# A spectral layer's last stage: tokens of a block spread over 128 partitions instead of 64

## The chip, the cores and the metric

The kernel runs on one core of a Trainium2 chip. The metric is the device time of one execution in microseconds (us); the kernel before took 10307.53 us, the median of three runs (10305.58 to 10308.48).

## The reference

Two layers of a "metaformer" work on `x` of shape (4, 64, 64, 128): 4 images, 4096 tokens each, 128 channels. Layer 0 is a selective-scan block and a mixture of experts; layer 1 is a message-passing block and a spectral one. Only the end of the last block matters here: a causal convolution of every channel with 16 filters along the tokens, done by discrete Fourier transforms, mixed by matrices, scaled, and added to its input.

```python
def _stu_conv(phi, u, n):
    Vf = jnp.fft.rfft(phi, n=n, axis=0)
    Uf_p = jnp.fft.rfft(u, n=n, axis=1)
    Uf_m = jnp.fft.rfft(u * sgn3, n=n, axis=1)
    U_plus = jnp.fft.irfft(Vf[None, :, :, None] * Uf_p[:, :, None, :], n=n, axis=1)[:, :sl]
    U_minus = jnp.fft.irfft(Vf[None, :, :, None] * Uf_m[:, :, None, :], n=n, axis=1)[:, :sl]
    ...
    for i, frac in enumerate((1, 2, 4, 8)):
        xi = x[:, :T // frac]
        si = _stu(xi, sigma, phi, M_u[i], M_phi_plus[i], M_phi_minus[i])
        ...
    return jnp.sum(stacked * weights, axis=-1)
...
t = t + _L1_ffn_ref(_ln_t(t), ...)
```

The weights are one-hot over the four lengths (all tokens, a half, a quarter, an eighth), so in the end each token's spectral result is multiplied by one number that depends only on which of four segments the token lies in.

## The kernel before, in words

The kernel first does the scans of the four images with everything else dealt in beside them, then the experts and sums of the last image, then `to_slots`, `spectrum()` (L1433) and `endings()` (L1586). `spectrum()` and `endings()` are the last calls.

The transform over 4096 tokens is split: a token's number is 64 times its block `j` (0 to 63) plus its position `p` in the block (0 to 63). `NB` = 64 blocks, `BP` = 64 positions, `NQ` = 64 frequencies with two parts each. `spectrum()` leaves in DRAM the array `zd` of shape (frequency q, part r, position p, image b, channel), 16.8 MB in float32; its last step (L1564) stores `zd` for the last two frequencies.

`endings()` undoes the transform over the blocks. For each position `p` it multiplies a constant matrix `gi_t` (128 rows: part and frequency; 64 columns: block) with the 128 x 512 slice of `zd` for that position (512 = 4 images x 128 channels), giving 64 blocks x 512 in PSUM. VectorE then multiplies by `wpj`, one number per block, and adds the block's residual `x3`; the sum goes to the output. It works in 16 groups of 4 positions:

- `load_x(g)` (L1596, DMAs at L1599): four DMAs, one per image, of 128 KB each. `mine` gives the rows: 64 blocks, each with 4 neighbouring tokens, 2 KB contiguous in DRAM. The tile `xr3` has the order (block, position, image, channel), so in SBUF each row falls apart into 512 B pieces.
- `load(g)` (L1601, DMAs at L1604): two DMAs of 512 KB, one per part, each onto 64 partitions of the tile `zb`, with 8 KB rows.
- `turn(g)` (L1609): four matmuls of 128 x 64 by 128 x 512 (L1612) and four `scalar_tensor_tensor` (L1614) on 64 partitions.
- `put(g)` (L1616, DMAs at L1618): four DMAs of 128 KB, back in the rows of `load_x`.

All these DMAs are issued on SP's queue, in an order that the framework's scheduler makes out of the loop: four x groups ahead, spectral loads two groups ahead of their use, puts one group behind. There are six `xr3` buffers, four `zb` buffers and eight PSUM banks. A seventh `load_x` reuses the first buffer and so waits for the first put to have landed, and so on.

`_dft_constants()` makes the matrices on the host: `gi_t`'s content and `seg`, a 64 x 4 mask that says which of the four segments each block lies in. `seg` is read in the tail of the filters' work, where it is multiplied by the segment weights and summed to `wpj` (L741 to L744).

Of the kernel before, what the change touches and what calls it, by code (L numbers as in the profile page):

```python
# [10 lines left out]
F32 = mybir.dt.float32  # L11
# [6 lines left out]
P = 128  # L18
B, H, W, C = 4, 64, 64, 128
# [21 lines left out]
BP = 64  # L41
NB = L // BP
NQ = NB
# [4 lines left out]
def _dft_constants():  # L48


    j, q = np.arange(NB)[:, None], np.arange(NQ)[None, :]
    th = 2 * np.pi / (2 * NB) * (j * q)
    one = (q == 0) & (j >= 0)
    alt = np.where(j % 2 == 0, 1.0, -1.0) * np.ones((1, NQ))
    co, si = np.cos(th), np.sin(th)
    fwd = np.stack([co, np.where(one, alt, -si)], 1)
    back = np.stack([np.where(one, 1.0, 2 * co), np.where(one, alt, -2 * si)], 1) / (2 * NB)
    gi = np.moveaxis(back, 0, 2)

    seg = np.zeros((NB, 4))  # L60
    for i in range(NB):
        seg[i, 0 if i < NB // 8 else 1 if i < NB // 4 else 2 if i < NB // 2 else 3] = 1.0
    r = fwd.reshape(NB, 2 * NQ), gi.reshape(2 * NQ, NB), seg
    return [np.ascontiguousarray(x.astype(np.float32)) for x in r]


# [35 lines left out]
def kernel(  # L102
# [35 lines left out]
    nc = tc.nc  # L138

    const = ctx.enter_context(tc.tile_pool(name="const", bufs=1))  # L140
# [3 lines left out]
    x3_d = [dram.tile([L, C], F32, name=f"x3_d{b}") for b in range(B)]  # L144
# [3 lines left out]
    zd = dram.tile([NQ, 2, BP, B, C], F32, name="zd")  # L148
# [64 lines left out]
    mu_t = wp.tile([P, 3, C], F32, name="mu_t")  # L213
    wseg = wp.tile([P, 4], F32, name="wseg")
    fu_c, gi_c, seg_c = _dft_constants()
    fq_c, gq_c = _twiddled()
    fq_d = nc.inline_tensor(fq_c, name="dft_in").ap()
    gq_d = nc.inline_tensor(gq_c, name="dft_out").ap()
    fu_t = wp.tile([NB, P], F32, name="fu_t")
    nc.sync.dma_start(fu_t, nc.inline_tensor(fu_c, name="dft_u").ap())  # L220
    gi_t = const.tile([P, NB], F32, name="gi_t")
    nc.sync.dma_start(gi_t, nc.inline_tensor(gi_c, name="dft_back").ap())
    wpj = const.tile([NB, 1], F32, name="wpj")

    eps5 = wp.tile([P, 1], F32, name="eps5")
    nc.vector.memset(eps5, 1e-5)
# [30 lines left out]
    def bank(shape, name):  # L257

        settle(1)
        return side["ones"].tile(shape, F32, name=name, tag="ps")  # L260
# [443 lines left out]
    def filters():  # L704

        with tc.tile_pool(name="fl", bufs=2) as fp:
# [30 lines left out]
            for s in range(2, -1, -1):  # L737
                nc.vector.tensor_add(
                    wseg[:, s : s + 1], wseg[:, s + 1 : s + 2], wt[:, 3 - s : 4 - s]
                )  # L740
            sg4 = fp.tile([NB, 4], F32, name="sg4")  # L741
            nc.sync.dma_start(sg4, nc.inline_tensor(seg_c, name="dft_seg").ap())
            nc.vector.tensor_mul(sg4, sg4, wseg[0:NB, :])
            nc.vector.reduce_sum(wpj, sg4, axis=AX.X)  # L744

            nc.scalar.activation(sg, sg, AF.Ln)
# [5 lines left out]
            for src, acc in ((m_plus, accp), (m_minus, accm), (m_u, mu_t)):  # L752
                n = src.shape[1]
                for i in range(4):
                    for k in range(0, n, 4):
# [4 lines left out]
                        h = hard[:, i : i + 1]  # L760
# [6 lines left out]
            for k in range(0, KF, 4):  # L767
# [11 lines left out]
                for a, m in enumerate((me, mo)):  # L779
                    ps = bank([P, 4, C], "mt_ps")  # L780
# [9 lines left out]
        with tc.tile_pool(name="hd_w", bufs=2) as hp:  # L790
# [21 lines left out]
            for k in range(0, KF, 4):  # L812
                ps = bank([BP, 4, 2, NQ], "h_ps")
                for i in range(4):
# [4 lines left out]
                        start=True,  # L819
                        stop=True,  # L820
# [11 lines left out]
            for q in range(0, NQ, 4):  # L832
# [5 lines left out]
                ps = bank([KK, 4, 2 * BP], "v_ps")  # L838
                for i in range(4):
                    for r in range(2):  # L840
# [4 lines left out]
                            start=(r == 0),  # L845
                            stop=(r == 1),
# [738 lines left out]

    def endings():  # L1586

        with tc.tile_pool(name="gi", bufs=3) as gp, tc.tile_pool(
            name="gi_ps", bufs=8, space=PSUM
        ) as gps:  # L1590
            zb, xr = {}, {}

            def mine(t, b, g):
                return t[b].rearrange("(j p) c -> j p c", j=NB)[:, 4 * g : 4 * g + 4, :]

            def load_x(g):  # L1596
                xr[g] = gp.tile([NB, 4, B, C], F32, name="xr3", bufs=6)
                for b in range(B):
                    nc.sync.dma_start(xr[g][:, :, b, :], mine(x3_d, b, g))  # L1599

            def load(g):  # L1601
                zb[g] = gp.tile([P, 4, B * C], F32, name="zb", bufs=4)
                for r in range(2):
                    nc.sync.dma_start(  # L1604
                        zb[g][r * NQ : (r + 1) * NQ],
                        zd[:, r, 4 * g : 4 * g + 4].rearrange("q p b c -> q p (b c)"),
                    )

            def turn(g):  # L1609
                for t in range(4):  # L1610
                    ps = gps.tile([NB, B * C], F32, name="gi_ps", tag="ps")
                    nc.tensor.matmul(ps, gi_t, zb[g][:, t, :], start=True, stop=True)  # L1612
                    xt = xr[g][:, t].rearrange("j b c -> j (b c)")
                    nc.vector.scalar_tensor_tensor(xt, ps, wpj, xt, ALU.mult, ALU.add)  # L1614

            def put(g):  # L1616
                for b in range(B):
                    nc.sync.dma_start(mine(out, b, g), xr[g][:, :, b, :])  # L1618

            for g in range(4):  # L1620
                load_x(g)
            n = BP // 4
            for g in range(n + 3):
                if g + 4 < n:
                    load_x(g + 4)
                if g < n:
                    load(g)
                if 0 <= g - 2 < n:
                    turn(g - 2)
                if 0 <= g - 3 < n:  # L1630
                    put(g - 3)

    def run(pieces):
        for _ in pieces:
# [3 lines left out]
    def beside(b):  # L1638

        if b == 0:  # L1640
            yield from before_scans(1)
            yield from before_scans(2)
            yield from gate(0)
            yield from gate(1)
            yield from filters()
            return
        if b == 2:
            yield from before_scans(3)
        yield from after_scans(b - 1)
        yield from experts_and_sums(b - 1)  # L1650
        yield from to_slots(b - 1)
        if b < B - 1:
            yield from gate(b + 1)

    with ExitStack() as c0:
# [113 lines left out]
        for s in range(-5, total + 2):  # L1769
            i = max(s, 0) // N  # L1770

            t = s + 5
# [8 lines left out]
            t = s + 3  # L1781
# [11 lines left out]
            if 0 <= s < total:  # L1793
                b, k, step, _ = chunks[i]
                n = s % N
# [44 lines left out]
            t = s - 1  # L1840
# [9 lines left out]
            t = s - 2  # L1850
            if t < 0:
                continue
            c, n = divmod(t, N)
            k = chunks[c][1]
            if n == 0:
                y = ys[c] = bps.tile([P, 4, 2, P], F32, name="y")
                if k == 0:
                    for q in range(4):
                        for h in range(2):
# [4 lines left out]
                                start=(q % 2 == 0 and h == 0),  # L1864
                                stop=False,
                                skip_group_check=True,
                            )
            for q in range(4):
                if q == 2:
                    deal(i_sp, i_act, i_pool, i_pe, i_dve)  # L1870
                for h in range(2):
# [5 lines left out]
                        start=(n == 0 and k > 0 and q % 2 == 0 and h == 0),  # L1877
                        stop=(n == N - 1),
# [31 lines left out]
    weights.close()  # L1910
    spectrum()
    endings()


# [72 lines left out]
```

## Time and profile before

| | us |
|---|---|
| median of three runs | 10307.53 |
| the profiled execution | 10298.26 |
| its span | 10296.2 |
| PE busy | 7631.4 (74% of the span) |
| DVE busy | 8537.4 (83%) |
| ACT busy | 6159.3 (60%) |
| POOL busy | 6493.4 (63%) |
| first DMA issue of `endings()` | at 10139.1 |
| first matmul of `endings()` | at 10161.5 |
| last VectorE instruction | at 10289.4 |
| 64 matmuls of L1612 (128 records) | 592 ns median a record |
| 64 instructions of L1614 | 743 ns median |
| DMA issue on SP at L1599, L1604, L1618 | 0.615, 0.614, 0.618 us median |

The profile is that of one execution. Busy shares are means over the whole span; stages differ, so a stage is read from the windows that cover it. A window's line gives busy time and count of each engine, then TensorE's granted clock as a share of full speed, the mean busy share of the 16 DMA engines (it can pass 1, since packets overlap), and what they moved in GB/s. A wait's line gives who waited, on what, how long in total, how often, and the longest.

### The profile page before, as it was taken

The numbers are of one execution on the slowest core, as the hardware profiler recorded it, in microseconds if no ns is written. First come the engines' busy times: TensorE is split into PE (matmuls) and PEld (weight loads), VectorE is DVE, ScalarE is ACT, GpSimd is POOL, SyncE is SP. The second block draws the span as 40 slices with busy tenths as digits, with TensorE's granted clock in tenths as the row PEclk, the third lists the DMA queues.
The fourth block names the chain that finished last, engine by engine and source line by source line (L and its number), as shares of the span: only waits on it lengthen the run. The fifth ranks groups of instructions, "written<-read, shape, count | busy, mean of one in ns | idle before, by whom it ended". The sixth has DMA issues, their size and how long they took to land. (4 is left out here: it accounts for less than half of the span.)

```text
span 10296.2 us, 137906 instructions
## 1 busy us (share of the span) xinstructions
PE 7631.4 (74%) x45570; PEld 4960.9 (48%) x45570; DVE 8537.4 (83%) x7103; ACT 6159.3 (60%) x11847; POOL 6493.4 (63%) x5948
## 2 busy tenths in 40 slices
PE   7676777667767767787767776767777767999996
PEld 3444444445543545444544554543555445666662
DVE  0899999989999999998999999999999951555553
ACT  4665766656755566675765666765576644554551
POOL 1677777878877778877877788877788741000000
PEclk9787787768777878788878887868877776999998
DMA  2556556657656645656756656756646663233336
GB/s 90 169 170 207 178 187 212 191 180 225 196 172 202 214 155 174 200 180 207 250 173 225 202 162 218 232 167 219 213 155 199 193 215 95 80 87 86 87 87 161
DMA packets 941918, 1806.03 MB, mean 175 GB/s; under 512 B 88184, under 2 KB 506648, under 8 KB 937624
## 3 DMA queue, kind: packets, MB, share of 16 engines
q1 hardware_dynamic: 941208, 1797.22, 54.7%
q8 instruction: 366, 6.00, 0.2%
q14 instruction: 344, 2.82, 0.1%
HBM read 1554.66 MB, written 242.22 MB: 175 GB/s over the span
## 5 line engine op out<-in xcount | busy, mean ns | idle before, releaser
L1846 POOL TENSOR_TENSOR hh<-hh,bc 128x1024 f32<-128x1024 f32 x2048 | 4886.8, 2386 | 384.9 <-DVE hh L1836 151.0
L1836 DVE TENSOR_TENSOR_SCAN hh<-da,hst,db 128x512 f32<-128x512 f32 x3584 | 4393.1, 1267 | 281.5 <-PE y L1872 30.1
L1872 PE MATMUL y<-ident,hh 128*128 128x128 f32 x16384 | 2723.2, 321 | 1524.8 <-POOL hh L1846 1429.0
L1786 ACT ACTIVATE da<-dl,aneg 128x512 f32<-128x512 f32 x4096 | 2781.8, 717 | 1543.7 <-DVE hh L1836 1531.2
L1872 PEld LDWEIGHTS y<-ident,hh 128*128 128x128 f32 x16384 | 2259.0, 166 | 2486.4 <-POOL hh L1846 1868.7
L1830 DVE TENSOR_TENSOR db<-du,bc 128x1024 f32<-128x1024 f32 x1920 | 2365.2, 1232 | 97.7 <-ACT du L1767 19.2
L1845 POOL COPY hst<-hh 128x2 f32<-128x2 f32 x1792 | 365.9, 204 | 1037.9 <-DVE hh L1836 937.0
L1495 PE MATMUL sp_ps<-vt,taps 32*128 32x256 f32 x8192 | 638.1, 405 | 52.3 <-DVE wt L1509 19.7
L1836 DVE TENSOR_TENSOR_SCAN hh<-da,db 128x512 f32<-128x512 f32 x512 | 597.0, 1208 | 38.4 <-PE y L1872 5.8
L1495 PEld LDWEIGHTS sp_ps<-vt,taps 32*128 32x128 f32 x8192 | 438.1, 185 | 245.6 <-DVE wt L1506 63.0
L440 PE MATMUL cv_ps<-xh,diag 128*128 128x512 f32 x1152 | 525.8, 599 | 1.8 <-ACT sg_v L382 0.9
L1524 PE MATMUL sp_ps<-wt,ut 128*32 128x256 f32 x8192 | 448.7, 379 | 45.2 <-DVE wt L1509 22.7
L1830 DVE TENSOR_TENSOR db<-dx,bc 128x1024 f32<-128x1024 f32 x128 | 179.3, 1401 | 297.9 <-POOL dx L1714 285.8
L1686 PE MATMUL dt_ps<-dts,dtw 8*128 8x512 f32 x512 | 378.9, 844 | 52.8 <-ACT sg_v L382 35.5
L1506 DVE COPY wt<-sp_ps 128x1024 f32<-128x1024 f32 x257 | 314.4, 1223 | 123.6 <-PE sp_ps L1495 112.2
L1509 DVE COPY wt<-sp_ps 128x1024 f32<-128x1024 f32 x255 | 311.3, 1221 | 121.9 <-PE sp_ps L1495 115.4
L1711 PE MATMUL dl_ps<-ex,ident 128*128 128x512 f32 x512 | 315.3, 704 | 121.9 <-POOL ex L1705 121.8
L1524 PEld LDWEIGHTS sp_ps<-wt,ut 128*32 128x32 f32 x8192 | 318.7, 110 | 172.6 <-ACT wt L1506 28.7
L1705 POOL TENSOR_TENSOR ex<-ex,dx 128x1024 f32<-128x1024 f32 x128 | 302.0, 2360 | 107.6 <-DMA bc<-bc_d 72.5
L1509 ACT COPY wt<-sp_ps 128x1024 f32<-128x1024 f32 x257 | 260.2, 1012 | 178.4 <-PE sp_ps L1495 169.4
L1456 DVE COPY zs<-sp_ps 128x1024 f32<-128x1024 f32 x128 | 156.5, 1222 | 241.8 <-PE sp_ps L1524 235.6
L1714 POOL TENSOR_TENSOR dx<-dl,xc 128x1024 f32<-128x1024 f32 x128 | 302.5, 2363 | 69.3 <-ACT dl L1712 62.8
(289 smaller groups left out, 9915.6 us busy)
## 6 DMA issues: line engine op xcount, KB each, us to landing
bc<-bc_d SPq DMA_DIRECT2D x2048, 512.0 KB
xc<-xc_d SPq DMA_DIRECT2D x128, 512.0 KB
y_d<-ys SPq DMA_DIRECT2D x128, 512.0 KB
w1t<-in_w_dram SPq DMA_DIRECT2D x96, 512.0 KB
w2t<-in_w_dram SPq DMA_DIRECT2D x192, 256.0 KB
xc_x<-xc_d SPq DMA_DIRECT2D x64, 512.0 KB
yk<-y_d SPq DMA_DIRECT2D x128, 256.0 KB
yk<-y_d SPq DMA_DIRECT2D x256, 128.0 KB
```

The lines of the kernel that those rows point to most:

```text
L440: nc.tensor.matmul(ps, diag[:, h, t, :], xh[:, 8 * g + dy : 8 * g + dy + 8, dx : dx + W], start=(t == 0), stop=(t == 8),)
L1495: nc.tensor.matmul(woven if (g // 2 + j) % 2 else plain, taps[rows, j, t, :], vt[i][rows].rearrange("k s n -> k (s n)"), start=True, stop= ...
L1509: copy()(dst, src)
L1524: nc.tensor.matmul(ps[32 * g : 32 * g + 32, k // 2, (k % 2) * 256 :][:, 0:256], w0.rearrange("d m u b -> d (m u b)"), wt[:, :, n : n + 2, ...
L1686: nc.tensor.matmul(ps, dtw[:, k, h * P : (h + 1) * P], dts, start=True, stop=True)
L1711: nc.tensor.matmul(ps, ident, t[:, h], start=t is dl, stop=t is w)
L1786: i_act = nc.scalar.activation(das[t][:, h, :], sizes[t // N][0][:, h, :], AF.Exp, scale=aneg[:, tk, h, t % N : t % N + 1],)
L1830: nc.vector.tensor_mul(db, src, bcs[s][:, 0:1, :].to_broadcast([P, 2, SC]))
L1836: i_dve = nc.vector.tensor_tensor_scan(o, d0, d1, init, ALU.mult, ALU.add)
L1845: nc.gpsimd.tensor_copy(hsts[t // N][:, :, t % N], hhs[t][:, :, last])
L1846: i_pool = nc.gpsimd.tensor_mul(hhs[t], hhs[t], bcs.pop(t)[:, 1:2, :].to_broadcast([P, 2, SC]))
L1872: i_pe = nc.tensor.matmul(ys[c][:, q, h, :], hhs[t][:, h, q * P : (q + 1) * P], ident, is_transpose=True, start=(n == 0 and k > 0 and q % ...
```

## The change

The output of the inverse transform is laid over 128 partitions instead of 64. The 64 positions of a block are cut into two halves h of 32; partition 2j + h holds block j's half h. A group now takes 4 positions of either half, 8 in all, so there are 8 groups instead of 16.

- `gi_t` grows from (128, 64) to (128, 2, 128): for each half a matrix whose 64 columns stand on the even or odd columns, zeros elsewhere. Two matmuls that accumulate into one PSUM bank, one per half, make one 128 x 512 result.
- `seg`, `sg4` and `wpj` are given for 128 partitions.
- `xr3` has the order (partition, image, position, channel), so that a DMA of `load_x` or `put` moves one contiguous 2 KB row per partition on both sides, 256 KB in all.
- `zb` holds both halves: a DMA of `load` moves 1 MB onto 64 partitions, two 8 KB rows each.
- The loop puts `load(g)` ahead of `load_x(g)`, both three groups ahead of the use; `put(g)` follows the loads of group g + 3. The pool is made with `reuse_waits="tile"`.

```diff
-    seg = np.zeros((NB, 4))
+    seg = np.zeros((NB, 2, 4))
     for i in range(NB):
-        seg[i, 0 if i < NB // 8 else 1 if i < NB // 4 else 2 if i < NB // 2 else 3] = 1.0
-    r = fwd.reshape(NB, 2 * NQ), gi.reshape(2 * NQ, NB), seg
+        seg[i, :, 0 if i < NB // 8 else 1 if i < NB // 4 else 2 if i < NB // 2 else 3] = 1.0
+    r = fwd.reshape(NB, 2 * NQ), np.zeros((2 * NQ, 2, NB, 2)), seg.reshape(P, 4)
+    for h in range(2):
+        r[1][:, h, :, h] = gi.reshape(2 * NQ, NB)
...
-    gi_t = const.tile([P, NB], F32, name="gi_t")
-    nc.sync.dma_start(gi_t, nc.inline_tensor(gi_c, name="dft_back").ap())
-    wpj = const.tile([NB, 1], F32, name="wpj")
+    gi_t = const.tile([P, 2, P], F32, name="gi_t")
+    nc.sync.dma_start(
+        gi_t, nc.inline_tensor(gi_c.reshape(P, 2, P), name="dft_back").ap()
+    )
+    wpj = const.tile([P, 1], F32, name="wpj")
...
-            sg4 = fp.tile([NB, 4], F32, name="sg4")
+            sg4 = fp.tile([P, 4], F32, name="sg4")
             nc.sync.dma_start(sg4, nc.inline_tensor(seg_c, name="dft_seg").ap())
-            nc.vector.tensor_mul(sg4, sg4, wseg[0:NB, :])
+            nc.vector.tensor_mul(sg4, sg4, wseg)
...
-        with tc.tile_pool(name="gi", bufs=3) as gp, tc.tile_pool(
+        with tc.tile_pool(name="gi", bufs=3, reuse_waits="tile") as gp, tc.tile_pool(
...
             def mine(t, b, g):
-                return t[b].rearrange("(j p) c -> j p c", j=NB)[:, 4 * g : 4 * g + 4, :]
+                return t[b].rearrange("(jh g t) c -> g jh t c", jh=P, t=4)[g]
 
             def load_x(g):
-                xr[g] = gp.tile([NB, 4, B, C], F32, name="xr3", bufs=6)
+                xr[g] = gp.tile([P, B, 4, C], F32, name="xr3", bufs=6)
                 for b in range(B):
-                    nc.sync.dma_start(xr[g][:, :, b, :], mine(x3_d, b, g))
+                    nc.sync.dma_start(xr[g][:, b], mine(x3_d, b, g))
 
             def load(g):
-                zb[g] = gp.tile([P, 4, B * C], F32, name="zb", bufs=4)
+                zb[g] = gp.tile([P, 2, 4, B * C], F32, name="zb", bufs=4)
                 for r in range(2):
                     nc.sync.dma_start(
                         zb[g][r * NQ : (r + 1) * NQ],
-                        zd[:, r, 4 * g : 4 * g + 4].rearrange("q p b c -> q p (b c)"),
+                        zd[:, r].rearrange("q (h g t) b c -> g q h t (b c)", h=2, t=4)[g],
                     )
 
             def turn(g):
                 for t in range(4):
-                    ps = gps.tile([NB, B * C], F32, name="gi_ps", tag="ps")
-                    nc.tensor.matmul(ps, gi_t, zb[g][:, t, :], start=True, stop=True)
-                    xt = xr[g][:, t].rearrange("j b c -> j (b c)")
+                    ps = gps.tile([P, B, C], F32, name="gi_ps", tag="ps")
+                    for h in range(2):
+                        nc.tensor.matmul(
+                            ps, gi_t[:, h, :], zb[g][:, h, t, :], start=(h == 0), stop=(h == 1)
+                        )
+                    xt = xr[g][:, :, t, :]
                     nc.vector.scalar_tensor_tensor(xt, ps, wpj, xt, ALU.mult, ALU.add)
 
             def put(g):
                 for b in range(B):
-                    nc.sync.dma_start(mine(out, b, g), xr[g][:, :, b, :])
-
-            for g in range(4):
-                load_x(g)
-            n = BP // 4
-            for g in range(n + 3):
-                if g + 4 < n:
-                    load_x(g + 4)
-                if g < n:
-                    load(g)
-                if 0 <= g - 2 < n:
-                    turn(g - 2)
-                if 0 <= g - 3 < n:
-                    put(g - 3)
+                    nc.sync.dma_start(mine(out, b, g), xr[g][:, b])
+
+            n = BP // 8
+            for g in range(3):
+                load(g)
+                load_x(g)
+            for g in range(n):
+                turn(g)
+                if g + 3 < n:
+                    load(g + 3)
+                    load_x(g + 3)
+                put(g)
```

## The prediction

> **What bounds the kernel now.** The change touches only the last stage, `endings()`, so I looked for its stretch of the span and for what limits it there. The page's forty slices show the last stage as about half a slice at the end; the windows by stage give it exact edges: first SP issue of L1599 at 10139.1 us, end of the span at 10296.2 us, that is 157 us or 1.5% of the span. Two windows of it (columns: busy time and count of PE, PEld, DVE, ACT, POOL, then PE clock, DMA share, GB/s):
>
> ```profile
> 10136.00:10167.00 31.00, 5.31 (x8) 1.39 (x8) 2.67 (x5) 0.00 (x0) 0.00 (x0) 0.56 0.97 182
> 10167.00:10290.00 123.00, 72.56 (x120) 19.52 (x120) 45.02 (x61) 0.00 (x0) 0.00 (x0) 0.81 0.90 227
> ```
>
> PE is busy 73 of 123 us and DVE 45; the DMA engines are busy 0.90 to 0.97 of the time, yet move only 182 and 227 GB/s. So this stage is bound by its DMAs. Next the DMA queue's own waits from 10120 us on:
>
> ```profile
> SPq L1599 <- DMA out_dram<-xr: 28.2, 16, 6.9
> ...
> SPq L1618 <- DVE xr L1614: 8.5, 5, 4.1
> SPq L1604 <- DMA zb<-zd: 4.3, 3, 2.0
> ```
>
> SP stood 28.2 us before an x load whose buffer was being written out by the put issued just ahead of it. And what was moved (DMA view of 10130 to 10297 us):
>
> ```profile
> DMA packets 37674, 34.15 MB, mean 204 GB/s; under 512 B 2594, under 2 KB 35362, under 8 KB 35622
> ...
> zb<-zd SPq DMA_DIRECT2D x32, 512.0 KB
> xr<-x_d SPq DMA_DIRECT2D x64, 128.0 KB
> out_dram<-xr SPq DMA_DIRECT2D x64, 128.0 KB
> ```
>
> Nearly all packets are 512 B pieces of x and out; the 16.8 MB of `zb` travel in some 2,000 packets of 8 KB. Last, the price of each kind. In 10141 to 10151 us only x loads are in flight, in 10165 to 10175 almost only `zb` loads, and in 8460 to 8500, in an earlier stage, expert weights `w_t`, 2 KB rows onto 128 partitions:
>
> ```profile
> 10141.00:10151.00 10.00, 0.00 (x0) 0.00 (x0) 0.00 (x0) 0.00 (x0) 0.00 (x0) 0.50 1.04 185
> 10165.00:10175.00 10.00, 6.53 (x16) 1.78 (x15) 5.25 (x8) 0.00 (x0) 0.00 (x0) 1.00 1.01 214
> 8460.00:8500.00 40.00, 35.90 (x384) 25.71 (x377) 1.23 (x3) 2.46 (x4) 0.00 (x0) 1.00 1.05 387
> ```
>
> All three with the DMA engines full: 185, 214 and 387 GB/s. The shape sets the rate.
>
> [...] 214/185 = 1.16 in the trace. [...] `zd` rows lie 256 KB apart, so that could also be behind the 214. `ub<-u_d`, 64 partitions at a pitch of 32 KB, ran at about 210 GB/s too[...]. The change keeps both for `zb`.
>
> **The change part by part**, against the profiled span (10296.2 us; that execution took 10298.26 us, the runs' median is 10307.53, so I carry the difference over to the median).
>
> *Layout of x and out.* Each becomes 8 groups of 4 DMAs (32 of 256 KB instead of 64 of 128 KB), 128 partitions, 2 KB contiguous on both sides. Loads: 8.39 MB at 185 GB/s = 45.3 us before, at 387 = 21.7 after. The 16 KB pitch of the new rows is that of `xc_d`, whose rows the scan loads all along. Stores: the last puts alone moved 0.52 MB in 2.8 us, so about 185 GB/s = 45.3 us; after, no row here shows 2 KB stores alone. Bounds: 21.7 us (as the loads) and 45.3 (no gain). I take 21.7, because a store's shape changes as a load's does.
>
> *`zb`.* 16 DMAs of 1 MB instead of 32 of 512 KB, still 64 partitions and 8 KB packets: 16.78 MB at 214 = 78.4 us, before and after.
>
> *Sum.* Before 45.3 + 45.3 + 78.4 = 169.0 us; the stage really moved its data from 10141 to 10294.3 = 153.3 us, 0.91 of the sum, stalls included. So mixing small x and out transfers between the `zb` halves gains something. After: 21.7 + 21.7 + 78.4 = 121.8. Now the two `zb` halves stand back to back, as they do in the 214 window, so I grant half of that discount: 0.95 x 121.8 = 116 us. Bounds 110 and 122.
>
> *SP order.* Issues fall from 160 to 80: 160 at some 0.62 us are 99 us; after, 64 over 128 partitions (0.36 us each for such x_d stores near 8640 us) and 16 at up to 1 us make 39 us, hidden under the DMAs. x loads now go into a buffer emptied three groups earlier, so the 28.2 us of waits go. In the built program each DMA takes one of eight completion semaphores in turn, so an issue waits for the DMA eight before it. When `load(g+3)` waits, seven of 256 KB are behind it: 1.8 MB, 4.7 us at 387 GB/s, against 3.4 to 3.9 us from issue to landing of a put in the chain of waits. Just covered: I add 3 us for bubbles over the stage and the last turn (bounds 0 and 8).
>
> *PE.* 64 instructions of 512 columns as before: 32 outputs with two accumulating instructions each, in place of 64 with one; 592 ns median per record, two records each. The weights become 128 wide; LDWEIGHTS of that width are 0.34 us at half clock in L1559 and lie under matmuls. A group of 16 records takes 7.2 us warm and up to 13.2 cold (3.62 and 6.6 us for 8 in the timeline). [...] the windows show 0.50 to 1.00 within groups. Groups come every 116/8 = 14.5 us, so PE stays hidden. If DMA took under 13 us a group, cold matmuls would show.
>
> *DVE.* 32 of about 743 ns (128 partitions, still 512 elements) instead of 64: 47.6 to 24 us, hidden both times, worth nothing but the last 0.75.
>
> *Start.* Both kernels wait there for the last `zd` store, since `load(0)` reads it. Spectral loads first merely reorder a full queue: `turn(0)` can start near 10155 instead of 10161.5, but PE is not the bound, so nothing. `gi_t` grows from 32 to 128 KB ahead of the first x tiles: 96 KB at about 190 GB/s = 0.5 us at most, I take 0.3. The mask `dft_seg` is nothing. On every engine the built instructions before this stage stand in the same order.
>
> Stage after: 10139.1 + 1.9 to the first data + 116 + 3 + 1.9 from last data to the end (10294.3 to 10296.2 before) = 10261.9. Gain 34.3 - 0.3 = 34 us; 10307.5 - 34 = **10273 us**.
>
> **Rivals.** (1) *Relief:* `zb` speeds up too, since its even and odd halves now follow each other[...]. Against it: the 214 window is exactly such alternation. All at 387 GB/s gives 87 us of DMA, stage end near 10233, time 10244; half of that effect, 10258. (2) *Smaller gain:* stores stay at 45.3 us, or bubbles at the upper bound: + 0.95 x 23.6 = 22 us, time 10295; with bubbles of 8 us and no discount, about 10286. For it: stores alone at 2 KB are not shown. (3) *Slower:* the ring of eight semaphores runs the DMA queue dry once per group. It holds 4.7 us; if landing and reissue took 9.0 us, 8 x 4.3 us would eat the gain, and from 11.5 us on the kernel is over 20 us slower, 10328. The only landing of that length (10.2 us for the first put) was queueing behind 4 MB of `zb`, so this is unlikely. (4) *The bound lies elsewhere:* a DMA stage with the wrong limit read; then within 20 us of 10307.
>
> **How the numbers follow.** A measurement of this kernel can hardly tell less than 0.2%, 20.6 us, so faster means under 10286.9. Forecast 0.66 (10258 to 10286), relief 0.14 (10241 to 10258), smaller gain 0.14, of which 0.05 under the border, rival 4 0.02, slower 0.04. Faster: 0.66 + 0.14 + 0.05 = 0.85; same 0.11; slower 0.04. Range for 8 in 10: 10254 to 10290, which takes in part of relief and the better part of the smaller gain.
>
> **What would show it.** Right: the stage some 123 us long; a DMA share near 1 at about 285 GB/s; packets under 2 KB gone; SP's waits on `out_dram<-xr` no longer of several us per group. PE's first matmul of a group waits for `zb` throughout. If `zb` stretches show over 300 GB/s, relief. If the DMA share dips once per group, the ring. If the DVE or PE have no idle time, I misread the limit. Wrong: a difference outside 10139 to the end, other than 0.3 us.

## The result and the profile after

The changed kernel took 10276.3 us, the median of seven runs (10270.5 to 10282.77), beside 10308.48 us before (seven runs); the ratio of the times is 0.9967, with a 95% interval of 0.9956 to 0.9979. So it is faster by about 32 us.

The profiled execution took 10273.64 us and its span is 10271.6 us. The changed stage can be cut out of it: it begins with the first issue on SP of `endings()`, at 10143.1 us, and ends with the span. That is 128.5 us, against 157.1 before (10139.1 to 10296.2): 28.6 us less. The start of the stage itself was 4 us later than before. Over all the profiles below it lies anywhere from 10139 to 10153 us, with nearly the same work ahead of it, so I compare the stage's length, which does not carry that scatter, and use the medians to confirm. Each ratio below is to runs of the kernel before that belong to the same set of runs: their median is 10313.86 us for the first four experiments and 10311.66 us for the last three, so an experiment's median is not to be set against the 10276.3 us above. The gains by these medians lie within 4 us of the gains in the stage. A stage's length comes from one profile of each kernel, and the 95% intervals of the ratios reach 6 to 13 us to either side, so a step of 7 to 9 us between two experiments rests on those single profiles.

The windows view of the changed kernel, over the inner part of the stage (columns as before: busy time and count of PE, PEld, DVE, ACT, POOL, PE clock, DMA share, GB/s), and two short stretches of it, one in which only `zb` is in flight, one in which only puts are:

```profile
10147.00:10268.00 121.00, 74.51 (x128) 30.54 (x128) 24.03 (x32) 0.00 (x0) 0.00 (x0) 0.76 1.02 266
...
10148.00:10154.00 6.00, 0.00 (x0) 0.00 (x0) 0.00 (x0) 0.00 (x0) 0.00 (x0) 0.50 1.02 208
...
10259.00:10263.00 4.00, 4.00 (x9) 1.69 (x8) 1.50 (x2) 0.00 (x0) 0.00 (x0) 0.83 1.05 405
```

The DMA engines are full all the time, at 266 GB/s instead of 227. `zb` moves at 208 GB/s, much as before (214). The puts, in rows of 2 KB from 128 partitions, move at 405. DVE's work has halved and PE's is the same.

The DMA view from 10130 us on (the first row is the busy share of 40 slices in tenths):

```profile
DMA  7003999999999999999999999999999999999961
...
DMA packets 12112, 35.14 MB, mean 246 GB/s; under 512 B 1349, under 2 KB 1368, under 8 KB 10062
...
zb<-zd SPq DMA_DIRECT2D x16, 1024.0 KB
xr<-x_d SPq DMA_DIRECT2D x32, 256.0 KB
out_dram<-xr SPq DMA_DIRECT2D x32, 256.0 KB
```

There is no dip between start and end. The 512 B packets are gone: 1,368 packets are under 2 KB where 35,362 were. SP's own waits show what SP now waits for:

```profile
SPq L1625 <- DMA zb<-zd: 44.0, 10, 4.8
SPq L1603 <- DMA zb<-zd: 25.8, 6, 5.9
...
SPq L1625 <- DMA out_dram<-xr: 3.9, 11, 0.7
SPq L1603 <- DMA out_dram<-xr: 3.2, 7, 0.9
```

The long waits are for a load of `zb` far ahead in the ring of eight semaphores, while the DMA engines are full, so I count them as costing nothing. The wait of an x load for the put just issued, 28.2 us before, is 3.2 us.

PE's timeline shows one burst of 16 records per group, each after a wait for `zb`:

```profile
10211.19 9.48 PE L1617 MATMUL gi_ps<-zb,gi_t 128*128 128x512 f32 x16 [6.61 <-DMA zb<-zd]
10226.39 8.72 PE L1617 MATMUL gi_ps<-zb,gi_t 128*128 128x512 f32 x16 [5.71 <-DMA zb<-zd]
```

Nine microseconds of work in a group of 15, so PE has 6 us to spare.

### The profile page after: what moved, and what is told of

It reads as the page before. It is cut to its first block, busy times and chain, and to the rows that moved or that the text cites. A ratio compares the mean times of both kernels' runs of the same rounds, so it can differ in the third digit from the quotient of the medians.

```text
span 10271.6 us, 137721 instructions
## 1 busy us (share of the span) xinstructions
PE 7612.8 (74%) x45570; PEld 4955.4 (48%) x45570; DVE 8512.7 (83%) x7071; ACT 6159.5 (60%) x11847; POOL 6494.2 (63%) x5948
## 5 line engine op out<-in xcount | busy, mean ns | idle before, releaser
L1528 PEld LDWEIGHTS sp_ps<-wt,ut 128*32 128x32 f32 x8192 | 317.9, 110 | 173.4 <-ACT wt L1510 28.6
```

The source lines that it names most:

```text
L1528: nc.tensor.matmul(ps[32 * g : 32 * g + 32, k // 2, (k % 2) * 256 :][:, 0:256], w0.rearrange("d m u b -> d (m u b)"), wt[:, :, n : n + 2, ...
```

## The experiments

The prediction's theory is that the DMA engines bound the stage, and that each kind of transfer has a rate which its shape in SBUF sets: how many partitions it reaches, and how long its pieces are (185, 214 and 387 GB/s in its three windows). The rivals are that the order of the issues was the cost, that the row length alone was, and, for `zb`, that its pitch in DRAM is.

### zb on all 128 partitions

```diff
-        r[1][:, h, :, h] = gi.reshape(2 * NQ, NB)
+        r[1][:, h, :, h] = gi.transpose(1, 0, 2).reshape(2 * NQ, NB)
...
-                for r in range(2):
+                for h in range(2):
                     nc.sync.dma_start(
-                        zb[g][r * NQ : (r + 1) * NQ],
-                        zd[:, r].rearrange("q (h g t) b c -> g q h t (b c)", h=2, t=4)[g],
+                        zb[g][:, h],
+                        zd.rearrange("q r (h g t) b c -> h g (q r) t (b c)", h=2, t=4)[h, g],
                     )
```

> The changed kernel with the 128 rows of zb taken in the order (frequency, part), so that one load covers all 128 partitions (two loads of 1 MB per group, one for each half), the rows of the constant matrix permuted to match. Theory (rate set by partitions): zb at 387 instead of about 213 GB/s, 43.4 instead of 78.8 us, the stage about 35 us shorter, some 93 us in all, time near 10241; the engines of PE then have less than 2 us idle per group. Rival (the 256 KB pitch of zd's rows in DRAM, or DRAM itself, holds zb at 213): the row pitch is now 128 KB, still a power of two, the stage stays within 5 us of 128.5 us. Second rival (PE becomes the bound): eight groups of 9.5 us and a start of 12 us, about 95 us, which hides in the same number, but the DMA share would fall under 0.9.

Measured: 10245.29 us (five runs), ratio to before 0.9935 (0.9922 to 0.9947), and a stage of 88.1 us (10151.1 to 10239.2). The windows view and PE's timeline of this kernel:

```profile
10152.00:10236.00 84.00, 62.28 (x128) 25.32 (x128) 22.72 (x32) 0.00 (x0) 0.00 (x0) 0.91 1.03 395
```

```profile
10173.63 7.11 PE L1617 MATMUL gi_ps<-zb,gi_t 128*128 128x512 f32 x16 [0.65 <-DMA zb<-zd]
10181.29 7.11 PE L1617 MATMUL gi_ps<-zb,gi_t 128*128 128x512 f32 x16 [0.55 <-DMA zb<-zd]
```

The same bytes now move at 395 GB/s, the mean over 84 us. The stage is 40 us shorter than in the changed kernel, 5 us more than I expected, and the DMA share stays at 1.03, so PE is not the bound, although it idles little. This version beats both kernels. With the DMA engines full at 395 GB/s, and no stretch quoted here above 405, I would look next for fewer bytes or an earlier start for some of them.

### The same 64 partitions, another pitch in DRAM

The step above also changed the distance between the rows in DRAM. This one changes that alone, by two unused rows behind each frequency:

```diff
-    zd = dram.tile([NQ, 2, BP, B, C], F32, name="zd")
+    zd = dram.tile([NQ, 2 * BP + 2, B, C], F32, name="zd")
...
-                        zd[:, r].rearrange("q (h g t) b c -> g q h t (b c)", h=2, t=4)[g],
+                        zd[:, r * BP : (r + 1) * BP].rearrange(
+                            "q (h g t) b c -> g q h t (b c)", h=2, t=4
+                        )[g],
```

> The changed kernel with two unused rows of 2 KB after each frequency of zd, so that the loads of zb still go to 64 partitions but step 260 KB instead of 256 KB in DRAM. Theory (partitions): windows with zb alone stay at 205 to 220 GB/s, stage 128.5 us within 3. Rival (power-of-two pitch): zb at up to 387 GB/s, stage near 93 us.

Measured: a stage of 128.1 us (10146.0 to 10274.1), 10286.59 us (six runs), ratio 0.9974 (0.9962 to 0.9985). In a window with little but `zb`:

```profile
10151.00:10158.00 7.00, 0.00 (x0) 0.00 (x0) 0.00 (x0) 0.00 (x0) 0.00 (x0) 0.50 0.98 201
```

The pitch of 256 KB was not the cause: with rows 260 KB apart `zb` moved at 201 GB/s, at 256 KB at 208. Of what the step above changed, the number of partitions that one load reaches is then the likeliest cause; the pitch of 128 KB and the new order in which rows are read came with it, and no run separates them. The loads of `zb` onto 64 partitions ran at 201 to 214 GB/s, while stores from 64 partitions ran at 320 to 340 GB/s (under "Puts on two queues"). So the 64 partitions look like a limit of loads here and not of stores; why is open.

### 512 B pieces on 128 partitions

```diff
-                xr[g] = gp.tile([P, B, 4, C], F32, name="xr3", bufs=6)
+                xr[g] = gp.tile([P, 4, B, C], F32, name="xr3", bufs=6)
...
-                    nc.sync.dma_start(xr[g][:, b], mine(x3_d, b, g))
+                    nc.sync.dma_start(xr[g][:, :, b, :], mine(x3_d, b, g))
...
-                    nc.sync.dma_start(mine(out, b, g), xr[g][:, b])
+                    nc.sync.dma_start(mine(out, b, g), xr[g][:, :, b, :])
```

> The changed kernel, but xr3 in the order (partition, position, image, channel) as before, so that x and out reach 128 partitions in pieces of 512 B. It tells packet size from partitions. Theory as worked out in the prediction [...]: x and out at about 330 GB/s, 51 instead of 43 us, stage 8 us longer, about 136 us. If all of the gain came from the partitions: no longer. If all of it came from the row length: stage near 170 us, as before or worse.

Measured: a stage of 136.5 us (10139.2 to 10275.7), 8.0 us longer than the changed kernel's, as the theory had it; 10294.66 us (nine runs), ratio 0.998 (0.9971 to 0.9989). Its puts, in a stretch of puts alone:

```profile
10267.00:10271.00 4.00, 1.22 (x3) 0.19 (x1) 1.04 (x2) 0.00 (x0) 0.00 (x0) 1.00 1.15 344
```

344 GB/s against 405 for 2 KB rows is a factor of 1.18. The prediction read 1.16 from the trace, as 214/185; from the 387 GB/s of `w_t` that makes an estimated 334 for x and out, beside the 330 expected.

### The new order with the old layout

```diff
-            for g in range(4):
-                load_x(g)
             n = BP // 4
-            for g in range(n + 3):
-                if g + 4 < n:
-                    load_x(g + 4)
...
+            for g in range(3):
+                load(g)
+                load_x(g)
+            for g in range(n):
+                turn(g)
+                if g + 3 < n:
+                    load(g + 3)
+                    load_x(g + 3)
+                put(g)
```

The pool also takes `reuse_waits="tile"`, as in the change; what that does by itself was not measured.

> The kernel before with its layout on 64 partitions and groups of 4 positions, but the new loop alone: spectral loads first, three groups ahead, each put after the loads of a later group, pool with waits by tile. Theory (rates by shape): the summed DMA time stays 169 us less some mixing, stage 150 to 165 us, time 10300 to 10315. Rival (the 28 us of SP waits for the put just issued were the cost): stage near 130 us, time near 10281.

Measured: a stage of 148.1 us (10152.8 to 10300.9), 9.0 us less than before; 10301.78 us (twelve runs), ratio 0.9987 (0.9979 to 0.9996). This is 2 us below the range that I had for the theory, and far from the rival's 130. The windows view and the first of SP's waits:

```profile
10157.00:10298.00 141.00, 84.27 (x128) 22.31 (x128) 46.36 (x64) 0.00 (x0) 0.00 (x0) 0.78 1.10 231
```

```profile
SPq L1618 <- DMA zb<-zd: 26.8, 23, 1.8
```

The waits of x loads for puts fall from 28.2 to 0.5 us and the DMA share rises from 0.90 to 1.10, but full engines in the old shapes move only 231 GB/s. The 28.2 us of SP's waits were worth 9.0 us. That the engines still had queued work for most of that time fits their share of 0.90 before; it is argued from that share.

### 2 KB rows on 64 partitions

```diff
-                xr[g] = gp.tile([NB, 4, B, C], F32, name="xr3", bufs=6)
+                xr[g] = gp.tile([NB, B, 4, C], F32, name="xr3", bufs=6)
...
-                    nc.sync.dma_start(xr[g][:, :, b, :], mine(x3_d, b, g))
+                    nc.sync.dma_start(xr[g][:, b], mine(x3_d, b, g))
...
-                    nc.sync.dma_start(mine(out, b, g), xr[g][:, :, b, :])
+                    nc.sync.dma_start(mine(out, b, g), xr[g][:, b])
```

> The kernel before with xr3 in the order (block, image, position, channel), so that x and out move rows of 2 KB, still onto 64 partitions and in the old order of issues. Theory (64 partitions hold any long row near 213 GB/s, as zb): x loads 39 instead of 45 us, stores at most as much less, the stage 145 to 153 us instead of 157. Rival (the length of the rows is what counted): x and out at 387 GB/s, stage near 120 us.

Measured: a stage of 149.5 us (10151.7 to 10301.2), 7.6 us less than before; 10302.48 us (twenty runs), ratio 0.9992 (0.9985 to 0.9998). Long rows alone bring about what they bring on 128 partitions (8.0 us), far from the rival's 37. But this run does not price loads of 2 KB rows onto 64 partitions. While x loads alone were in flight, SP issued 128 KB every 0.63 us, which is 207 GB/s; just that was moved, and the DMA engines were not full (share 0.68):

```profile
10154.00:10164.00 10.00, 0.00 (x0) 0.00 (x0) 0.00 (x0) 0.00 (x0) 0.00 (x0) 0.50 0.68 207
```

### The changed layout with the old order

The changed kernel with the loop of before, for 8 groups, and without `reuse_waits="tile"`.

> The changed kernel's layout with the old loop (x loads first and four groups ahead, puts one group behind, pool without waits by tile). If the order is worth as much here as it was alone (9 us): stage near 137 us. Theory: with 8 groups and six xr3 buffers only two x loads meet a put just issued, so at most two such waits of some 3 to 7 us, and the DMA engines stay full: stage 128 to 134 us.

Measured: a stage of 135.3 us (10144.0 to 10279.3), 6.8 us more than the changed kernel; 10286.37 us (twelve runs), ratio 0.9977 (0.9969 to 0.9986). My range of 128 to 134 was too low; the other case that I had named, an order worth as much as it was alone, had 137. SP's waits:

```profile
SPq L1603 <- DMA out_dram<-xr: 24.6, 4, 14.7
SPq L1625 <- DVE xr L1621: 14.4, 2, 7.7
```

There were fewer waits for a put, but each was longer, up to 14.7 us, probably since groups are twice as large. So the new order is worth 9.0 us with the old layout and 6.8 us with the new one, and the layout brings the other 20 to 22 of the 28.6.

### Puts on two queues

This one tests the prediction's price of the old stores, 185 GB/s, which was read from the last puts of the kernel before.

```diff
-                    nc.sync.dma_start(mine(out, b, g), xr[g][:, :, b, :])
+                    (nc.scalar if b % 2 else nc.sync).dma_start(mine(out, b, g), xr[g][:, :, b, :])
```

> The kernel before with the puts of two of the four images issued by ScalarE's queue, which is idle in this stage. It tells whether the 185 GB/s of the last puts, from which the prediction priced the stores, was the DMA engines' rate or SP's issue of 128 KB every 0.66 us (198 GB/s). Engines' rate: the last stretch, in which only puts are in flight, stays near 185 GB/s. Issue: it goes to 250 GB/s or more. The stage: 145 to 157 us.

Measured once: 10312.73 us, a stage of 162.1 us (10148.5 to 10310.6), longer and not shorter, where I had 145 to 157. The very last puts, in 10306.5 to 10309 us, still ran at 182 GB/s with half of them issued elsewhere, so SP's issue was not what held them:

```profile
10306.50:10309.00 2.50, 0.00 (x0) 0.00 (x0) 0.00 (x0) 0.00 (x0) 0.00 (x0) 0.56 0.94 182
```

But 10 us earlier, when the puts that had queued behind the last `zb` loads came through, the same kind of put ran nearly twice as fast. The rows of the DMA view for 10296 to 10298 us, in slices of 50 ns:

```profile
GB/s 358 379 51 225 92 82 103 113 144 123 144 195 154 215 256 287 287 297 307 338 338 338 338 359 338 338 338 338 358 348 318 348 348 348 338 359 338 338 348 328
DMA packets 1066, 0.55 MB, mean 275 GB/s; under 512 B 68, under 2 KB 1061, under 8 KB 1061
```

Of 1,066 packets 1,061 are under 2 KB and no load of x is left, so these are puts of 512 B pieces from 64 partitions, at about 340 GB/s. The kernel before did the same. In this stretch, 10283 to 10284 us, its queued puts are alone too:

```profile
DMA packets 663, 0.32 MB, mean 320 GB/s; under 512 B 38, under 2 KB 663, under 8 KB 663
```

The last puts are thus no measure of what the puts cost inside the stage. Why a fresh put is slower than a queued one, these runs do not show. SP's waits for puts grew (L1599 34.8 us and L1618 20.3 us in all), which would explain the longer stage; that is argued, not tested.

## Why the prediction was right, and where it was not

**The limit and the sign** held, and so did the rate of `zb` by its shape: 208 GB/s onto 64 partitions, 395 in the mixed stage with it on 128. The forecast was 10273 us, the median is 10276.3; the gain by medians is 32 us where 34 was forecast. The stage itself is 128.5 us, where the prediction had 122.8, so the gain in it is 28.6 us; its DMA engines moved 266 GB/s where about 285 was forecast. That the medians came closer to the forecast than the stage did is scatter, and so luck.

**Layout of x and out.** 387 GB/s was taken for both. The stores, which no row of before showed, ran at 405 in a stretch of their own: the lower bound of their time was the right one to take. The 185 GB/s of the old loads was read as a rate of full DMA engines; the window behind it is a mixture. At first SP's issue set the rate (128 KB every 0.66 us is 199 GB/s, and the share is 0.69); then the engines were full, at 178:

```profile
10141.00:10143.00 2.00, 0.00 (x0) 0.00 (x0) 0.00 (x0) 0.00 (x0) 0.00 (x0) 0.50 0.69 196
10147.00:10151.00 4.00, 0.00 (x0) 0.00 (x0) 0.00 (x0) 0.00 (x0) 0.00 (x0) 0.50 1.25 178
```

**`zb`** was priced unchanged at 214 and moved at 208 in its stretch. Its cause, taken to be the 64 partitions, stood against the rival pitch.

**Sum** is the step that failed, by 6 us. The bare sum of the three kinds was 121.8 us. From before's 169 against 153 I had read that mixing small and large transfers gains 9%, and granted half of it, "0.95 x 121.8 = 116". The 169 was too high, above all because the old stores stood in it at 185 GB/s, the rate of the last puts; at the 340 that queued puts reach they cost 24.7 us, and the sum is 45.3 + 24.7 + 78.4 = 148.4, below the 153.3 that was measured with SP's waits in it.

The packet records in the traces show the same more directly. I add up the durations of one kind of packet over the stage and divide by the 16 engines. Before, x and out took 69.3 us, not 90.6: from 10180 to 10290 us, 85% of their packets took 24 to 30 ns, as the queued puts did (27), where the x loads of 10145 to 10151 us took 55. `zb` took 70.8 us, not 78.4: its packets lasted 552 ns on the mean, against 612 where `zb` was alone. So the old mixture was cheap, for `zb` too. In the changed kernel `zb` took 77.9 us, at 608 ns a packet: nothing of it was handed on, and the discount should have been nought.

Without the discount the prediction's own terms give 1.9 + 121.8 + 3 + 1.9 = 128.6 us for the stage; it measured 128.5. Part of that agreement is luck: x and out took 49.4 us by their packets where 43.4 was priced, and the 3 us of bubbles in the sum do not show in the DMA row.

**SP order.** "The 28.2 us of waits go" is right. That the order was worth 9.0 us alone (6.8 in the new layout) was not in the working as a term of its own; it was hidden in the ratio 0.91. The sentence that spectral loads first are worth nothing has not been tested by itself: the experiment moved the whole loop.

**PE and DVE** stayed hidden: 8.5 to 9.9 us of PE a group (7.2 to 13.2 forecast) in 15 us, and DVE 24.0 us at 751 ns each.

**Start.** 0.3 us was forecast for the larger `gi_t`. The first ACT instruction on x stands at 12.78 us instead of 12.50.

**Rivals.** Relief did not come: the window of `zb` alone shows 208 GB/s, and the 40 us that faster `zb` loads are worth came only when its rows were put elsewhere. The sum in the second rival was a little off: bubbles of 8 us and no discount add 5 + 5.8 us to 10273, which is 10284 and not 10286. Slower by the ring of eight: no slice of the stage dips.

In sum, each step by one profile, and the first three on the way to the changed kernel: the order (with the pool's `reuse_waits`) 157.1 to 148.1 us; then the spread over 128 partitions, still in 512 B pieces, to 136.5; then 2 KB rows to 128.5; then `zb` on 128 partitions too, to 88.1. The last step was not part of the change, and is worth more than all of it. The second step also halves the number of groups and doubles every DMA. If stores from 64 partitions were fast before, its 11.6 us come from the loads; no run spreads the loads alone.

## What to carry to other kernels

Where a stage's DMA engines are full and the GB/s are low, price each kind of transfer from a window in which it is alone, then look at its shape: loads onto 64 partitions ran at 178 to 214 GB/s here with the engines full, `w_t` in 2 KB rows onto 128 at 387. Check first that the engines are full in that window; if they are not, it may show the rate of issue (196 to 207 GB/s at a share of 0.68 to 0.69 here). A split that needs two half-width loads can, as that of `zb` here, be interleaved on the partitions instead: that took 40 us off the stage and cost no more than a permuted constant matrix. The last transfers of this kernel ran without a queue behind them, and were a poor price for those inside it.

## What the runs showed of the hardware that was not expected

Stores in 512 B pieces from 64 partitions moved at about 340 GB/s when queued, as fast as the same pieces from 128 partitions (344), though loads of 512 B onto 64 partitions moved at 178 with the engines full. Unqueued, these stores ran at 182. And with `zb` on 128 partitions the stage kept 395 GB/s over 84 us of mixed loads and stores, above the 387 of weight loads from which the prediction's first rival had its 87 us.
